# A mixture-of-experts layer on Trainium2: token rows moved by indirect transfers through tables in DRAM, where one-hot products moved them

## The chip, the core and the metric

The kernel runs on one core of one Trainium2 chip. The core has five engines with a queue each: TensorE (PE) for matrix products, VectorE (DVE), ScalarE (ACT), GpSimd (POOL) and SyncE (SP), which only issues transfers. Results of TensorE land in PSUM banks; DVE and ACT read them from there. Transfers are issued from the queue of SP, ACT or POOL and run on 16 shared DMA engines. All data is float32. The metric is the device time of one execution in microseconds (us).

## The reference

Sixteen batches of 64 latent rows (1024 rows of 256 features) go through a two-layer Perceiver: cross-attention, self-attention and a forward layer, then cross-attention over a context of 1024 rows per batch ("L1 xattn"), self-attention ("L1 attn"), and a mixture of experts ("L1 ffn"). The change touches the last:

```python
def _L1_ffn_ref(x, Wr, W1, W2):          # x after _layernorm
    B, S, D, F, E = (8, 512, 256, 1024, 8)
    t = b * s                            # 1024 tokens
    cap = max(math.ceil(t * CAPACITY_FACTOR / E), 1)     # 128
    xf = x.reshape(t, d)
    probs = jax.nn.softmax(xf.astype(jnp.float32) @ Wr, axis=-1)
    eidx = jnp.argmax(probs, axis=-1)
    p_tok = jnp.take_along_axis(probs, eidx[:, None], axis=1)[:, 0]
    onehot = jax.nn.one_hot(eidx, E, dtype=jnp.int32)
    rank_all = jnp.cumsum(onehot, axis=0) - onehot
    rank = jnp.take_along_axis(rank_all, eidx[:, None], axis=1)[:, 0]
    keep = rank < cap
    ...
    xe = xf[dispatch]                    # (8, 128, 256)
    h = jnp.maximum(jnp.einsum('ecd,edf->ecf', xe, W1), 0.0)
    ye = jnp.einsum('ecf,efd->ecd', h, W2)
    ye = ye * (pe * valid.astype(ye.dtype))[:, :, None]
    y = jnp.zeros((t, d), dtype=x.dtype).at[dispatch.reshape(-1)].add(ye.reshape(E * cap, d).astype(x.dtype))
...
x = x + _L1_ffn_ref(_layernorm(x, axis=-1), L1_ffn_Wr, L1_ffn_W1, L1_ffn_W2)
```

Each token goes to the one expert with the highest probability. An expert takes the first 128 tokens that chose it; a token past that keeps its x unchanged.

## The kernel before

The 1024 rows are eight tiles of 128 partitions, held in `xs` for the whole kernel. The stages run one after the other, and each hides work of its neighbours:

- The L0 stage (to about 1160 us) attends over the context and works on the small self-attention of earlier tiles between.
- The L1 loop (`NSTEP` = 64 steps, eight to a token tile, about 12 us a step) attends over the context again. Each step softens the scores of 128 rows (`soften`, `turn_probs`), sends the turned probabilities over SP (`l_pT`), computes keys five steps ahead (`keys`: product, ACT copy, SP transfers `l_ks`, a POOL product at L876, a DVE sum at L877), and sums context rows by the probabilities (`gather`). `weave` lays the gather's products between the other items of the step.
- The L1 self-attention of a finished tile comes as 13 pieces (`make_self_pieces`: 0 norm, 1 turn, 2 to 5 queries and keys, 6 and 7 values, 8 scores and softmax, 9 and 10 turn, 11 attend, 12 output). `SELF_AT` says at which step of the loop each runs: pieces 0 to 7 in the second half of the following tile's steps, 8 to 12 in the first half of the one after. Tiles 6 and 7 finish after the loop, their pieces interleaved by hand with the routing of tiles 0 to 5.

From the L1 loop on every TensorE instruction is pinned (`in_order`, `pin`): TensorE runs them as written, so an instruction whose input is late holds all that follow. On the other engines the framework's scheduler puts the instructions in an order of its own, which then is fixed as well: each engine and each DMA queue works in order.

After the loop, the mixture layer: `route_norm(t)` (L1359) and `route(t)` (L1362) compute the normed rows and eight logits of a tile. When the last tile is done (L1415 to L1446), softmax, choice of expert and slot are computed for all tiles at once: a product with a triangle of ones gives ranks inside a tile, one with ones the counts of the tiles before. Then rows are moved by products with one-hot matrices: `m_send` (L1451, slot equals column) carries the normed rows to their experts (`m_px`, 64 products of 128x512), `m_back` (L1494, made of `m_pb` products) carries results home (`m_pz`, 128 products of 128x256). Per expert there are `m_ph` (hidden layer, ReLU on ACT) and `m_py`. `load_expert` (L1343) issues the two weight matrices of an expert on POOL's queue into the four buffers of `wpool`, two experts ahead.

Helpers named in the profile: `matmul` is L98, `transpose` L102, `copy` L111 (ACT) and L113 (DVE), `load_weight` L118, `inverse_std` L123 and L124, `layer_norm` L132 to L136, `turn_tile`'s copy L148.

Of the kernel before, what the change touches and what calls it, by code (L numbers as in the profile page):

```python
# [41 lines left out]
K6_TRI, K6_IOTA, K6_COL, K6_DESC, K6_SEL = 0, 128, 256, 257, 265  # L42
NK6 = 1289
# [3 lines left out]
def kernel(  # L47
# [9 lines left out]
    k6_in: bass.AP,  # L57
    x_wq: bass.AP,
# [124 lines left out]
    wpool = ctx.enter_context(tc.tile_pool(name="wbig", bufs=4))  # L183
    stc = ExitStack()
# [576 lines left out]
    with ExitStack() as st:  # L761
# [125 lines left out]
        def latents(t):  # L887

            rstd = two.tile([P, 1], F32, tag="ln_rstd", name=f"rstd_l_{t}")
            mv = mv_l.pop(t)
            nc.scalar.activation(rstd, mv[:, 1:2], AF.Sqrt, bias=eps2, scale=1.0 + EPS)
            nc.vector.reciprocal(rstd, rstd)
            xn[t] = one.tile([P, D], F32, tag="xn", name=f"l_xn_{t}")
            nc.vector.tensor_scalar(
                xn[t], xs[:, t, :], mv[:, 0:1], rstd, ALU.subtract, ALU.mult
            )

        def turn_latents(t):
            pt = bank([P, NC, P], f"lnT_l_{t}")
            for c in range(NC):
                transpose(pt[:, c, :], xn[t][:, c * P : (c + 1) * P], ident)
# [184 lines left out]

        SELF_AT = [(8,), (9, 10), (11,), (12,), (0,), (1, 2), (3, 4), (5, 6, 7)]  # L1090
# [4 lines left out]
        def self_pools():  # L1095

            wp = ws.enter_context(tc.tile_pool(name="s_w", bufs=4, side="right"))
            sw["pool"] = ws.enter_context(tc.tile_pool(name="s_one", bufs=1, side="right"))
            sw["ps"] = ps_s
            for name, w in (("q", s_wq), ("k", s_wk), ("v", s_wv), ("o", s_wo)):  # L1100
                sw[name] = load_weight(wp, w, f"w{name}5")

        def self_steps(s):
            t, at = divmod(s, PER_TILE)
            t -= 1 if at >= 4 else 2
            return [self_pieces(t)[n] for n in SELF_AT[at]] if t >= 0 else []
# [6 lines left out]
        def make_self_pieces(t, pool):  # L1113
# [98 lines left out]
            def self_output():  # L1212
# [7 lines left out]
                nc.gpsimd.tensor_tensor(xs[:, t, :], xs[:, t, :], v["xn"][:, 0, :], ALU.add)  # L1220
# [62 lines left out]
        for s in range(NSTEP):  # L1283
# [25 lines left out]
            if t + 1 < NT:  # L1309
# [6 lines left out]
                elif at == 5:  # L1316
                    items.append(lambda: queries(t + 1))
            w = (s - 2) // 2
# [8 lines left out]
        assert not pieces  # L1327
        for c in range(NC):
# [9 lines left out]
    NE, FF = m_w1.shape[0], m_w1.shape[2]  # L1338
# [4 lines left out]
    def load_expert(e):  # L1343
        return load_weight(wpool, m_w1[e], f"w1_{e}"), load_weight(wpool, m_w2[e], f"w2_{e}")

    with ExitStack() as st:
        one = st.enter_context(tc.tile_pool(name="m_one", bufs=1))
        two = st.enter_context(tc.tile_pool(name="m_two", bufs=2))
        k6 = one.tile([P, NK6], F32, tag="k6", name="k6")
        nc.sync.dma_start(out=k6, in_=k6_in)  # L1350
        wr = one.tile([P, NC, NE], F32, tag="wr", name="wr")
        nc.sync.dma_start(out=wr, in_=m_wr.rearrange("(c p) n -> p c n", p=P))
        experts = {e: load_expert(e) for e in range(2)}
        ones = one.tile([P, P], F32, tag="ones", name="ones")
        nc.gpsimd.memset(ones, 1.0)
        xn = one.tile([P, NT, D], F32, tag="xn", name="xn6")
        pl = one.tile([P, NT, NE], F32, tag="logits", name="m_logits")

        def route_norm(t):  # L1359
            layer_norm(two, xs[:, t : t + 1, :], xn[:, t : t + 1, :], f"m_{t}", 1)  # L1360

        def route(t):  # L1362

            hm = turn_tile(two, xn[:, t : t + 1, :], f"m_{t}")
            pr = bank([P, NE], f"m_logits_{t}")
            for c in range(NC):
                matmul(
                    pr, lhsT=hm[:, c, :], rhs=wr[:, c, :], start=(c == 0), stop=(c == NC - 1)
                )
            nc.vector.tensor_copy(pl[:, t, :], pr)  # L1370


        with ExitStack() as tail:
            ps_s = tail.enter_context(tc.tile_pool(name="s_ps", bufs=2, space=bass.MemoryType.PSUM))
            sw["ps"] = ps_s
            sp = tail.enter_context(tc.tile_pool(name="s_last", bufs=1))
            before, last = self_pieces(NT - 2), make_self_pieces(NT - 1, sp)
            last[0]()
            before[8]()
            last[1]()  # L1380
            for n in (2, 3):
                last[n]()
            before[9]()
            for n in (4, 5):
                last[n]()
            before[10]()
            last[6]()
            before[11]()
            last[7]()
            last[8]()  # L1390
            before[12]()
            for t in range(NT - 2):
                route_norm(t)
                route(t)
                if t == 2:
                    last[9]()
                if t == 4:
                    last[10]()
            last[11]()
            route_norm(NT - 2)  # L1400
            route(NT - 2)
            last[12]()
        ws.close()
        route_norm(NT - 1)
        route(NT - 1)
        one = st.enter_context(tc.tile_pool(name="m_big", bufs=1))

        def each(ap):
            return ap.unsqueeze(2).broadcast_to([P, NT, NE])

        red = one.tile([P, NT], F32, tag="red", name="m_red")
        prob = one.tile([P, NT, NE], F32, tag="prob", name="m_prob")
        top = one.tile([P, NT], F32, tag="top", name="m_top")
        hot = one.tile([P, NT, NE], F32, tag="hot", name="m_hot")
        nc.vector.tensor_reduce(red, pl, AX.X, ALU.max)  # L1415
        nc.vector.tensor_tensor(prob, pl, each(red), ALU.subtract)
        nc.scalar.activation(prob, prob, AF.Exp)
        nc.vector.tensor_reduce(red, prob, AX.X, ALU.add)
# [256 lines left out]
```

## Time and profile before

| what | us |
|---|---|
| time, median of 4 runs (lowest, highest) | 2185.66 (2182.41, 2187.97) |
| the profiled execution's own time | 2188.58 |
| its span, first to last instruction | 2186.8 |
| PE, DVE, ACT, POOL busy | 2094.7, 1323.1, 811.4, 311.5 |
| last of the latents' output added to xs | 1989.5 |
| last xs after self-attention | 2040.7 |
| first product of the first expert (m_ph) | 2082.8 |
| last product of m_py ends, about | 2156 |

In the profile a line such as `L98 PE MATMUL m_px<-m_send,xn` names the line of the program, the engine, the operation, and what is written from what. A float32 product is recorded as two matmuls. POOLq, SPq and DVEq are the issuing queues. "Idle before" is the time an engine stood still before the instruction, and `<-` names what ended it. PEclk is the granted clock of TensorE (1.00 is full).

### The profile page before, as it was taken

To read this page: it belongs to the slowest core of one execution; us is meant where nothing else is said; L and a number is where in the kernel's file an instruction comes from. 1 tells how busy PE (TensorE), PEld (TensorE's weight loads), DVE (VectorE), ACT (ScalarE), POOL (GpSimd) and SP (SyncE) were. 2 spreads that over 40 slices of the span, in tenths; PEclk is the share of its full clock that TensorE was granted. 3 is DMA by queue.
4 is the path that set the end of the run, shared out by engine and by line. 5 is a ranking of instruction groups with operands and counts; after the bars stand their busy time and mean duration, and the time that the engine had idled before them with its cause. 6 is when DMAs were issued, how large, how long until landed. Compare 5 with 4: busy or idle time off the path is not lost.

```text
span 2186.8 us, 30787 instructions
## 1 busy us (share of the span) xinstructions
PE 2094.7 (96%) x11016; PEld 1406.9 (64%) x11016; DVE 1323.1 (61%) x2606; ACT 811.4 (37%) x1567; POOL 311.5 (14%) x302
## 2 busy tenths in 40 slices
PE   7899999999999999999998799999999999998799
PEld 4567666667666666666665355666666666676477
DVE  5765656656566575575633768767666767664311
ACT  2222233333342233332434445454545545432110
POOL 2200001001000010010102232222121222211010
PEclk9999999999999999999998999999999999999799
DMA  7343333343333333444322355444444444332052
GB/s 245 87 105 97 84 81 99 85 108 75 83 102 97 74 99 79 109 111 108 79 78 77 80 165 136 106 119 104 103 112 102 116 98 113 95 88 84 0 180 71
DMA packets 150391, 220.48 MB, mean 101 GB/s; under 512 B 34704, under 2 KB 85392, under 8 KB 149984
## 3 DMA queue, kind: packets, MB, share of 16 engines
q1 hardware_dynamic: 142448, 188.00, 34.2%
q0 software_dynamic: 7792, 30.51, 4.1%
q8 instruction: 89, 1.46, 0.3%
q14 instruction: 62, 0.51, 0.1%
HBM read 67.38 MB, written 1.05 MB: 31 GB/s over the span
## 4 chain that ended last, share of the span: by engine, by line
PE 80%; DVE 6%; ACT 5%; issue 3%; SPq 3%; DMA 2%; POOL 1%; DVEq 0%; ACTq 0%; POOLq 0%
PE x_po L98 20%; PE x_s L98 19%; PE l_po L98 8%; PE l_pk L98 7%; PE l_s L98 2%; PE x_pa L98 2%; PE s_pq L98 1%; PE m_py L98 1%; PE m_px L98 1%; PE m_ph L98 1%; PE m_pz L98 1%; PE x_pq L98 1%; SPq L1015 1%; PE x_pv L98 1%; PE s_pk L98 1%
## 5 line engine op out<-in xcount | busy, mean ns | idle before, releaser
L98 PE MATMUL x_s<-ctxT,x_qk 128*128 128x512 f32 x1024 | 472.9, 603 | 10.6 <-ACT pr_x L584 10.6
L98 PE MATMUL x_po<-x_pT,ctx 128*128 128x256 f32 x2048 | 459.3, 382 | 4.2 <-DMA x_pT<-x_pb 4.2
L98 PEld LDWEIGHTS x_po<-x_pT,ctx 128*128 128x128 f32 x2048 | 388.6, 191 | 80.3 <-issue 26.6
L98 PEld LDWEIGHTS x_s<-ctxT,x_qk 128*128 128x128 f32 x1024 | 187.6, 191 | 211.2 <-issue 183.1
L577 DVE TENSOR_REDUCE nmax_x<-x_s 128x1 f32<-128x1024 f32 x128 | 156.0, 1218 | 240.6 <-PE x_s L98 239.6
L98 PE MATMUL l_pk<-l_cnT,wkv 128*128 128x512 f32 x512 | 247.3, 610 | 3.2 <-DVE a_vm L356 1.5
L584 ACT ACTIVATE pr_x<-x_s,shift_x 128x1024 f32<-128x1024 f32 x128 | 142.5, 1114 | 286.9 <-DVE shift_x L581 238.6
L98 PE MATMUL l_po<-l_pT,l_ctx 128*128 128x256 f32 x864 | 232.9, 385 | 7.8 <-DMA l_pT<-l_pb 4.4
L876 POOL TENSOR_TENSOR l_ks<-l_ks,k 128x512 f32<-128x512 f32 x128 | 166.2, 1320 | 424.5 <-DMA l_ks<-l_kr 345.7
L98 PEld LDWEIGHTS l_po<-l_pT,l_ctx 128*128 128x128 f32 x864 | 153.6, 191 | 77.5 <-issue 54.8
L98 PEld LDWEIGHTS l_pk<-l_cnT,wkv 128*128 128x128 f32 x512 | 95.9, 193 | 106.7 <-issue 87.4
L864 ACT ACTIVATE l_kr<-l_pk,l_bkv 128x512 f32<-128x512 f32 x128 | 87.5, 687 | 198.4 <-PE l_pk L98 135.3
L593 DVE STREAM_TRANSPOSE x_pb<-pr_x 128x1024 f32<-128x1024 f32 x128 | 157.3, 1237 | 5.9 <-DMA x_pT<-x_pb 1.9
L618 ACT COPY x_pct<-x_po 128x512 f32<-128x512 f32 x64 | 37.5, 585 | 246.6 <-PE x_po L98 246.6
L865 DVE TENSOR_TENSOR l_kT<-l_kr,k 128x512 f32<-128x512 f32 x128 | 96.2, 754 | 46.8 <-ACT l_kr L864 45.9
L178 DVE TENSOR_SCALAR pr_x<-pr_x,inv_x 128x1024 f32<-128x1024 f32 x128 | 100.2, 782 | 3.2
L983 DVE TENSOR_REDUCE nmax_l<-l_s 128x1 f32<-128x1024 f32 x64 | 75.8, 1219 | 35.6 <-PE l_s L98 35.6
L877 DVE TENSOR_TENSOR l_kT<-l_kT,l_ks 128x512 f32<-128x512 f32 x128 | 92.0, 760 | 4.1 <-POOL l_ks L876 4.1
L584 ACT ACT_TABLE_LOAD x42 | 53.9, 1283 | 105.7 <-DVE shift_x L581 105.6
L1006 DVE STREAM_TRANSPOSE l_pb<-pr_l 128x1024 f32<-128x1024 f32 x64 | 77.7, 1230 | 1.2 <-issue 0.6
L98 PE MATMUL l_s<-l_kT,l_qT 64*64 64x512 f32 x512 | 69.1, 625 | 8.0 <-DVE l_kT L877 8.0
L986 ACT ACTIVATE pr_l<-l_s,nmax_l 128x1024 f32<-128x1024 f32 x64 | 71.5, 1117 | 8.3 <-DVE nmax_l L984 8.0
(302 smaller groups left out, 2657.8 us busy)
## 6 DMA issues: line engine op xcount, KB each, us to landing
x_pT<-x_pb SPq DMA_DIRECT2D x1024, 64.0 KB, 2.0
l_ks<-l_kr SPq DMA_DIRECT2D x256, 128.0 KB, 2.3
l_pT<-l_pb SPq DMA_DIRECT2D x512, 64.0 KB, 2.0
ctx<-in_context_dram SPq DMA_DIRECT2D x32, 512.0 KB, 5.2
w<-in_m_w_dram POOLq DMA_DIRECT2D x16, 1024.0 KB, 5.9
ctxT<-x_cb SPq DMA_DIRECT2D x240, 64.0 KB, 2.0
l_ctx<-in_context_dram SPq DMA_DIRECT2D x27, 512.0 KB, 4.3
l_ctx_spare<-in_context_dram SPq DMA_DIRECT2D x5, 512.0 KB, 4.3
```

The source lines that it names most:

```text
L98: ins = nc.tensor.matmul(*args, **kwargs)
L178: nc.vector.tensor_scalar(pr, pr, inv, None, ALU.mult)
L577: nc.vector.tensor_reduce(nmax, sc, AX.X, ALU.max, negate=True)
L584: nc.scalar.activation(pr, sc, AF.Exp, bias=shift, scale=1.0, accum_out=total)
L593: nc.vector.transpose(blocks[w][:, :, i], pr.rearrange("p (j k s) -> p j k s", j=4, s=32))
L864: nc.scalar.activation(kr[:, i % 2], pk, AF.Identity, bias=bkv[:, i : i + 1])
L865: nc.vector.tensor_tensor(kr2, kr[:, i % 2], k4[:, 0, at], ALU.mult)
L876: nc.gpsimd.tensor_tensor(ks[:, i % 2], ks[:, i % 2], k4[:, 1, at], ALU.mult)
L877: nc.vector.tensor_tensor(kr2, kr2, ks[:, i % 2], ALU.add)
L983: nc.vector.tensor_reduce(nmax, sc[h], AX.X, ALU.max, negate=True)
L986: nc.scalar.activation(pr[h], sc[h], AF.Exp, bias=nmax, scale=1.0, accum_out=total[:, 2 * h : 2 * h + 1])
L1006: nc.vector.transpose(blocks[w][:, :, h].rearrange("p j k s -> p k j s"), pr[h].rearrange("p (k j s) -> p k j s", k=NKT, s=32),)
```

## The change

Routing moves into the L1 loop, tile by tile. `route_norm(t-2)` runs at step 4 of tile t's eight steps, `route(t-2)` at step 5 and a new `place(t-2)` at step 6; tiles 6 and 7 follow after the loop. `place(t)` finds the slot of each token of one tile (t products with ones for the tiles before, one with the triangle) and issues four indirect scatters on POOL's queue, one row per token: the normed row into the table `m_norm`, the probability and the token's number into `m_meta`, the row of `xs` into `m_rest`, all at row 128 x expert + rank; and for a token over capacity the row of `xs` straight to the output. Indices past the end (`NOWHERE`) are dropped. The tables are in DRAM and are filled at `open_routes` from a row of constants.

The experts' phase then reads the tables back with plain transfers (`xr` on ACT's queue, `mm` and `rr` on SP's), turns the rows of an expert on TensorE, computes the two layers one expert ahead, adds the kept rows on DVE and scatters 128 finished rows per expert to the output from POOL's queue. The one-hot matrices and their products are gone. Six experts' weights are loaded ahead, on SP's queue, with a new pool `w_more`; experts 6 and 7 reuse `wpool`. Tile 6's pieces 0 to 3 come two steps later and 4 to 7 after the loop's last step; the order of the last two tiles' pieces is another; the last tile's sum into `xs` runs on DVE.

```diff
+        def open_routes():
+            rt["x"] = one
+            rp = rt["pool"] = routes.enter_context(tc.tile_pool(name="m_route", bufs=1, side="right"))
+            rt["k6"] = rp.tile([P, NK6], F32, tag="k6", name="k6")
+            nc.sync.dma_start(out=rt["k6"], in_=k6_in)
+            rt["wr"] = rp.tile([P, NC, NE], F32, tag="wr", name="wr")
+            nc.sync.dma_start(out=rt["wr"], in_=m_wr.rearrange("(c p) n -> p c n", p=P))
+            rt["hot"] = rp.tile([P, NT, NE], F32, tag="hot", name="m_hot")
+            for name, at, n in (("norm", 0, D), ("rest", 0, D), ("meta", D, 2)):
+                rt[name] = mdram.tile([NTOK, n], F32, tag=name, name=f"m_{name}")
+                nc.gpsimd.dma_start(
+                    out=rt[name], in_=k7_in[:, at : at + n].broadcast_to([NTOK, n])
+                )
+
+        def route_norm(t):
+            rx[t] = rt["x"].tile([P, 1, D], F32, tag="xn", name=f"m_x_{t}")
+            layer_norm(rt["pool"], xs[:, t : t + 1, :], rx[t], f"m_{t}", 1)
+
+        def meta(t):
+            return rt["k6"][:, K6_META + 2 * t : K6_META + 2 * t + 2]
+        def route(t):
+
+            hm = turn_tile(rt["h"], rx[t], f"m_{t}")
+            pr = bank([P, NE], f"m_logits_{t}")
+            for c in range(NC):
+                matmul(
+                    pr, lhsT=hm[:, c, :], rhs=rt["wr"][:, c, :], start=(c == 0), stop=(c == NC - 1)
+                )
+            prob = rt["pool"].tile([P, NE], F32, tag="prob", name=f"m_prob_{t}")
+            nmax = small.tile([P, 1], F32, tag="nmax", name=f"m_nmax_{t}")
+            total = small.tile([P, 1], F32, tag="total", name=f"m_total_{t}")
+            top, hot = meta(t)[:, 0:1], rt["hot"][:, t, :]
+            desc = rt["k6"][:, K6_DESC : K6_DESC + NE]
+            nc.vector.tensor_reduce(nmax, pr, AX.X, ALU.max, negate=True)
+            nc.scalar.activation(prob, pr, AF.Exp, bias=nmax, scale=1.0, accum_out=total)
+            soft_norm(prob, total, f"m_{t}")
+            nc.vector.tensor_reduce(top, prob, AX.X, ALU.max)
+            nc.vector.scalar_tensor_tensor(hot, prob, top, desc, ALU.is_equal, ALU.mult)
+            nc.vector.tensor_reduce(total, hot, AX.X, ALU.max)
+            nc.vector.tensor_scalar(hot, desc, total, None, ALU.is_equal)
+
+        def place(t):
+
+            pool, hot = rt["pool"], rt["hot"]
+            pr = bank([P, NE], f"m_rank_{t}")
+            for k in range(t):
+                matmul(
+                    pr, lhsT=rt["k6"][:, K6_ONES : K6_ONES + P], rhs=hot[:, k, :],
+                    start=(k == 0), stop=False,
+                )
+            matmul(
+                pr, lhsT=rt["k6"][:, K6_TRI : K6_TRI + P], rhs=hot[:, t, :],
+                start=(t == 0), stop=True,
+            )
+            keep = pool.tile([P, NE], F32, tag="keep", name=f"m_keep_{t}")
+            at = pool.tile([P, NE], F32, tag="at", name=f"m_at_{t}")
+            one = small.tile([P, 2], F32, tag="one", name=f"m_one_{t}")
+            idx, idx2 = (
+                pool.tile([P, 1], mybir.dt.int32, tag=f"idx{k}", name=f"m_idx{k}_{t}")
+                for k in range(2)
+            )
+            nc.vector.scalar_tensor_tensor(
+                keep, pr, float(P), hot[:, t, :], ALU.is_lt, ALU.mult
+            )
+            nc.vector.tensor_tensor(at, pr, rt["k6"][:, K6_PLACE : K6_PLACE + NE], ALU.add)
+            nc.vector.tensor_tensor(at, at, keep, ALU.mult)
+            nc.vector.tensor_reduce(one[:, 0:1], at, AX.X, ALU.add)
+            nc.vector.tensor_scalar(idx, one[:, 0:1], NOWHERE, None, ALU.add)
+            nc.vector.tensor_reduce(one[:, 1:2], keep, AX.X, ALU.add)
+            nc.vector.tensor_scalar(
+                idx2, one[:, 1:2], NOWHERE, meta(t)[:, 1:2], ALU.mult, ALU.add
+            )
+            for k, dst, src in (
+                (idx, rt["norm"], rx.pop(t)[:, 0, :]), (idx, rt["meta"], meta(t)),
+                (idx, rt["rest"], xs[:, t, :]), (idx2, out, xs[:, t, :]),
+            ):
+                pin(nc.gpsimd.indirect_dma_start(
+                    out=dst, out_offset=bass.IndirectOffsetOnAxis(ap=k, axis=0),
+                    in_=src, in_offset=None, bounds_check=NTOK - 1, oob_is_err=False,
+                ))
...
         def self_steps(s):
             t, at = divmod(s, PER_TILE)
-            t -= 1 if at >= 4 else 2
-            return [self_pieces(t)[n] for n in SELF_AT[at]] if t >= 0 else []
+            items = []
+            if t >= 2 and at in (5, 6):
+                items.append(lambda: (route if at == 5 else place)(t - 2))
+            n = SELF_AT[at]
+            t1 = t - (1 if at >= 4 else 2)
+            if t1 == NT - 2:
+
+                n = {6: (0,), 7: (1, 2, 3)}.get(at, ())
+            return items + ([self_pieces(t1)[k] for k in n] if t1 >= 0 else [])
 
...
                 nc.vector.tensor_tensor(v["xn"][:, 0, :], po, v["xn"][:, 0, :], ALU.add)
-                nc.gpsimd.tensor_tensor(xs[:, t, :], xs[:, t, :], v["xn"][:, 0, :], ALU.add)
+
+                eng = nc.vector if t == NT - 1 else nc.gpsimd
+                eng.tensor_tensor(xs[:, t, :], xs[:, t, :], v["xn"][:, 0, :], ALU.add)
...
+            if t >= 2 and at == 4:
+                items.append(lambda: route_norm(t - 2))
...
+        for n in (4, 5, 6, 7):
+            self_pieces(NT - 2)[n]()
...
+    def load_expert(e, pool):
+        ws = []
+        for k, w in enumerate((m_w1[e], m_w2[e])):
+            ws.append(pool.tile([P, w.shape[0] // P, w.shape[1]], F32, tag="w", name=f"w{k + 1}_{e}"))
+            nc.sync.dma_start(out=ws[k], in_=w.rearrange("(c p) n -> p c n", p=P))
+        return ws
...
+        more = st.enter_context(tc.tile_pool(name="w_more", bufs=8))
+        experts = {e: load_expert(e, wpool if e < 2 else more) for e in range(6)}
...
+            rt["x"] = rt["h"] = two
             before, last = self_pieces(NT - 2), make_self_pieces(NT - 1, sp)
             last[0]()
             before[8]()
-            last[1]()
-            for n in (2, 3):
+            for n in range(1, 9):
                 last[n]()
-            before[9]()
-            for n in (4, 5):
+            for n in (9, 10, 11, 12):
+                before[n]()
+            route_norm(NT - 2)
+            for n in (9, 10):
                 last[n]()
-            before[10]()
-            last[6]()
-            before[11]()
-            last[7]()
-            last[8]()
-            before[12]()
-            for t in range(NT - 2):
-                route_norm(t)
-                route(t)
-                if t == 2:
-                    last[9]()
-                if t == 4:
-                    last[10]()
+            route(NT - 2)
             last[11]()
-            route_norm(NT - 2)
-            route(NT - 2)
+            place(NT - 2)
             last[12]()
+            route_norm(NT - 1)
+            route(NT - 1)
+            place(NT - 1)
...
+        xr = one.tile([P, NE, D], F32, tag="xr", name="m_xr")
+        rr = one.tile([P, NE, D], F32, tag="rr", name="m_rr")
+        mm = one.tile([P, NE, 2], F32, tag="mm", name="m_mm")
+        to = one.tile([P, NE], mybir.dt.int32, tag="to", name="m_to")
+        rows3 = rt["norm"].rearrange("(e p) d -> p e d", p=P)
+        for e0, e1 in ((0, 1), (1, 3), (3, NE)):
+            nc.scalar.dma_start(out=xr[:, e0:e1, :], in_=rows3[:, e0:e1, :])
+        nc.sync.dma_start(out=mm, in_=rt["meta"].rearrange("(e p) k -> p e k", p=P))
+        nc.sync.dma_start(out=rr, in_=rt["rest"].rearrange("(e p) d -> p e d", p=P))
+        nc.vector.tensor_copy(to, mm[:, :, 1])
+
...
+        turn_rows(0)
+        turn_rows(1)
+        hidden(0)
+        for e in range(NE):
+            hidden(e + 1)
+            turn_rows(e + 2)
+            w2 = experts.pop(e)[1]
...
+            res = two.tile([P, D], F32, tag="res", name=f"m_res_{e}")
             nc.vector.scalar_tensor_tensor(
+                res, py, mm[:, e, 0:1], rr[:, e, :], ALU.mult, ALU.add
+            )
+            nc.gpsimd.indirect_dma_start(
+                out=out, out_offset=bass.IndirectOffsetOnAxis(ap=to[:, e : e + 1], axis=0),
+                in_=res, in_offset=None, bounds_check=NTOK - 1, oob_is_err=False,
+            )
+            if e < 2:
+                experts[e + 6] = load_expert(e + 6, wpool)
```

## The prediction

> **What bounds the kernel now.** I read the page from the top, then the chain in order of time from 1975 us on, then a table by stretch, then the groups and waits of POOL and SP, which the change loads. The page gives one full engine:
>
> ```profile
> span 2186.8 us, 30787 instructions
> ...
> PE 2094.7 (96%) x11016; PEld 1406.9 (64%) x11016; DVE 1323.1 (61%) x2606; ACT 811.4 (37%) x1567; POOL 311.5 (14%) x302
> ...
> PEclk9999999999999999999998999999999999999799
> ```
>
> TensorE is busy 96% of the span; its clock drops only in the last slices. The table by stretch splits the L1 loop (1284 to 1984), the last two token tiles (to 2041), and the mixture layer after:
>
> ```profile
> 1284.00:1984.00 700.00, 681.25 (x4252) 455.24 (x4253) 470.98 (x847) 334.08 (x694) 160.84 (x133) 1.00 0.45 112
> 1984.00:2041.00 57.00, 45.01 (x476) 36.80 (x474) 26.64 (x75) 19.86 (x30) 8.10 (x9) 0.79 0.19 66
> ```
>
> Columns are length, then busy us of PE, PEld, DVE, ACT, POOL, then clock. In the loop PE idles 18.75 us of 700, so any product added there shows; DVE is at 67%. In the second stretch PE idles 12 us and its clock is 0.79: it waits on the last tiles' softmax. From there everything lies on one chain:
>
> ```profile
> 2043.42 0.63 PE m_logits L98 x4
> 2044.07 0.18 DVE m_logits L1370
> ...
> 2051.99 1.87 PE m_st L102 x8
> 2053.85 5.06 PE m_px L98 x10
> ...
> 2061.19 21.73 PE m_px L98 x50
> 2082.92 3.57 PE m_ph L98 x32
> 2086.49 1.91 PE m_pb L98 x4
> 2088.40 3.65 PE m_py L98 x16
> ...
> 2155.97 27.64 PE m_pz L98 x128
> 2183.63 0.48 DVE m_res L1515
> ```
>
> The experts' own products (m_ph, m_py) take 7.2 us each; m_px, m_pb and m_pz are the one-hot moving. POOL's rows and SP's waits, for the new transfers:
>
> ```profile
> L118 POOL DMA_DIRECT2D wk<-in_s_wk_dram x1 | 0.7, 721 | 0.0
> L118 POOL DMA_DIRECT2D wo<-in_s_wo_dram x1 | 0.9, 922 | 0.0
> L245 POOL DMA_DIRECT2D aw<-in_a_w_dram x1 | 0.5, 534 | 1.0 <-DMA wkT<-in_x_wk_dram 1.0
> L210 POOL MEMSET eps<- 128x1 f32 x1 | 0.1, 98 | 0.0
> ...
> POOL l_ks L876 <- DMA l_ks<-l_kr: 345.7, 45, 12.3
> ...
> SPq L873 <- DVE l_kT L877: 18.9, 11, 2.6
> ...
> out_dram<-m_res SPq DMA_DIRECT2D x8, 128.0 KB, 1.7
> ```
>
> POOL waits 345.7/45 = 7.7 us a step for l_ks: that is the room for its new work. SP already waits at times for the buffer that POOL's l_ks product helps to free.
>
> **What leaves the path.** After the last xs (2040.7): m_px, 2053.85 to 2082.92, 29.1; m_st 1.9; m_pb 8 x 1.91 = 15.3; m_pz 27.7; the batch routing from logits to slots, 2044.07 to 2051.99, 7.9. Sum 81.9 us. The DVE work that went with them (m_send 9.2, m_back 12.0) was hidden under PE and is worth nothing more.
>
> **What comes onto the path there.** Routing of the last tile, from logits to row index: maximum 0.25, table load 1.28 and exponential with its sum 0.5, some twelve small DVE steps at 0.23 (the m_hot, m_red rows), the rank product 0.5: 5.3. The first scatter's issue X, and its landing 2.0 (between 1.7, the out rows, and the 2.0 of the 64 KB moves). Reload of the first expert's rows from the table: 2.0. Two transposes and the copy, as lnT_m and hT_m ran: 1.2. Transposes of the rows for the six experts whose turn lies between products, 6 x 0.43: 2.6. PE starts the experts after an idle stretch: s_pq there took 3.78 and s_pk 2.72 instead of 1.95 at 1995 us: 2.6. The result leaves by a POOL scatter, X + 2.0, where SP took 2.7: X - 0.7. Sum 15.0 + 2X.
>
> X is one indirect scatter of 128 rows on POOL, and no row shows one. Lower end 0.53, the smallest plain transfer on POOL. Upper end: every row handled like an instruction of its own, 128 x 0.098 (the MEMSET of 128x1) = 12.5. I take 1.5: the row nearest in kind is the plain POOL transfer with 1 KB runs, 0.92, and reading the list of indices is added as one more such fixed start, 0.53. Stage net: 15.0 + 3.0 - 81.9 = -63.9.
>
> **The last two tiles (1984 to 2041).** Routing of tiles 0 to 5 leaves, but it filled the wait on tile 7's softmax; in its place come tile 6's turn, attention and output. Tile 7 still waits: tile 6's output, its norm, its route (transposes, copy, logits, 1.6) and its place sit ahead of tile 7's attention and output in PE's written order, and each needs DVE and ACT first, with Sqrt, Exp and Gelu tables (1.28 each) taking turns. Walking the order with these durations, tile 7's xs comes 3 us sooner. Bounds: 0 if each of these waits ends as late as now, 12 if PE's idle here goes. The last addition on DVE (0.42) rather than POOL (0.72) is in the 3. Pieces 4 to 7 of tile 6 now come after the loop, in front of the last gather: the same products, and the 1.3 us wait for l_pT at 1975 is filled.
>
> **The loop gains work.** For tiles 0 to 5: transposes 0.41 and logits 0.61, 6 x 1.02 = 6.1. `place(t)` has t+1 products of 128x8; two such take 0.61, so 21 x 0.305 = 6.4. In `route` the logits follow the transposes with only a DVE copy between: 0.52 where DVE was free (the m_logits rows), and about 0.7 more behind a busy DVE: 6 x 1.2 = 7.3. Sum 20 on PE, at worst all on the path; at best its 18.75 us of idle takes half: +10. DVE gets per tile norm 1.2, copy 0.42, seven steps of route and seven of place at 0.23, 4.8 in all, ACT two table loads, Sqrt and Exp, 3.4: I take nothing for them, since DVE (67%) and ACT (48%) have room under PE; without that cover they would cost up to 6 x 8.2 = 49.
>
> POOL gets four scatters per tile, pinned, and stands still until the indices come. Behind them on its queue are the next step's l_ks product and tile t+1's s_pr scaling; for l_ks wait DVE's key sum, then SP's next l_ks transfers and, in SP's order, l_pT, which PE's gather needs. 4X fits into 7.7 while X is under 1.9, so at 1.5 nothing is late. Above, 4 x 6 = 24 us per further us of X if all of it passes through.
>
> **At nothing.** The table fills (three POOL transfers, 0.9 each, once, in a 7.7 us gap). Constants and m_wr earlier on SP, 2 x 0.6, beside a wait of SP. Expert loads moved from POOL to SP: 16 issues of 0.6 with SP idle. Six experts' 12.6 MB start when the last latent products free the buffers, about 1990; at four loads in 18.0 us (the s_w loads) that is 54 us, 2044, while expert 0's are first and the others follow at 7.6 us each. At 5.9 us a load (the m_w rows) the last lands at 2061, when expert 5 starts past 2090. The reload on ACT's queue (three issues) waits behind nothing.
>
> **Sum.** 2186.8 - 63.9 - 3 + 20 = 2139.9. The profiled execution took 2188.58, 1.8 around its span, and stands 2.9 above the median 2185.66: forecast 2139.9 + 1.8 - 2.9 = 2139, 2.1% faster.
>
> **A rule against it.** POOL's rows show transfers beside DVE work at their normal 0.72 to 0.92, at 1284.8 to 1287.9, though the only DVE work beside them read PSUM. The Trainium skill, page SBUF — State Buffer, section "SBUF: two separate sides", says that a transfer issued from POOL can't write its descriptors while DVE runs an operation that takes both shared ports, and gives some 620 ns alone against some 3100 beside a DVE copy. By that, an estimate of X = 4.0 in the loop, the sum would be 2139 + 24 x 2.1 = 2189: no gain. I keep the row's view, since DVE's queue holds such operations only part of the time.
>
> **Rivals.**
> *Scatters dear on POOL (slower).* Place: POOL between two l_ks products. Each us of X above 1.9 costs 24 in the loop and 2 at the end. The gain of 46.7 is used up at X = 1.9 + 45.9/26 = 3.7. At 12.5: 254 in the loop, 22 at the end, and the experts run at POOL's 12.5 instead of PE's 7.6 (+39): 2139 + 315 = 2454. For it: no row shows X, POOL is in order, SP's waits show that l_ks is close. Against: 7.7 us of room, plain transfers under 1 us with eight times the runs.
> *Middle price.* X of 2 to 3.7, or copies and routing waiting on DVE and ACT: 2142 to 2186. For it: s_xn on DVE varied from 0.37 to 1.34 us, so DVE's queue is not free.
> *Loop covers more.* Half the 20 hidden and the 12 us of PE's idle before 2041 gone: 2139 - 10 - 9 = 2120. For it: 18.75 us of idle; against: PE's order is written by hand, and route stalls it.
> *No change.* The reload chain and the late routing eat all 82: it would take 47 us more than counted, 12 at the end and 35 in the loop; only the first rival offers that.
>
> **How the numbers follow.** A measurement of this kernel tells about 0.2% (4 us) from no change. Chances: main case, 2122 to 2155, 0.42; loop covers more, 2105 to 2122, 0.14; middle price, to 2181, 0.21; dear scatters, above 2190, 0.20; within 0.2%, 0.03. Faster 0.77, same 0.03, slower 0.20. For 8 in 10 the range takes the first three and the beginning of dear scatters (X to about 4.7): 2105 to 2212; the likeliest alone has 2122 to 2155.
>
> **What would show it.** Right: m_px, m_pb, m_pz gone, experts' products 7.6 us apart; first m_ph some 14 us after the last xs; L1 loop about 20 us longer with POOL's scatter rows near 1.5; l_ks products no later than now. Wrong: scatter rows above 2 us; PE waiting for l_pT or l_kT after each `place`; waits of PE on hT_m in the loop above 2 us; POOL, not PE, setting the distance between experts.

## The result and the profile after

The changed kernel takes 2190.84 us (median; 2185.9 to 2195.72) where the kernel before, measured beside it, takes 2187.78 (2181.54 to 2195.03). The ratio is 1.0015 with a 95% interval of 1.001 to 1.002: no gain, where 2.1% was forecast and 2139.0 us. The profiled execution took 2189.98 us, with a span of 2188.2.

The page of the kernel after, the lines that answer to those of before:

```profile
span 2188.2 us, 30690 instructions
...
PE 2039.0 (93%) x10868; PEld 1378.1 (63%) x10868; DVE 1317.0 (60%) x2666; ACT 817.5 (37%) x1582; POOL 337.5 (15%) x327
...
PE   5599999999999999999998888999999999999868
...
PEclk8799999999999999999998999999999999999879
DMA  9533334334333343344433246544444443433621
```

and the same two rows of the kernel before:

```profile
PE   7899999999999999999998799999999999998799
DMA  7343333343333333444322355444444444332052
```

TensorE does 56 us less, as meant, and the span is 1.4 us longer. So some 57 us of new idle time must be found. The first row shows most of it without any further view: PE has 5, 5 in its first two slices (0 to 109 us), where before it had 7, 8. Nothing of the mixture layer was meant to run there.

The table by stretch of the kernel after (length, busy us of PE, PEld, DVE, ACT, POOL, then clock, share of the DMA engines' time, GB/s); the last two rows are the L1 loop and the last two tiles, cut at the same work as in the forecast's table:

```profile
0.00:30.00 30.00, 19.63 (x102) 15.74 (x103) 9.39 (x35) 6.28 (x20) 13.07 (x22) 0.89 0.95 338
30.00:60.00 30.00, 12.34 (x61) 6.28 (x59) 4.58 (x11) 3.63 (x12) 0.00 (x0) 0.77 1.12 88
60.00:100.00 40.00, 22.25 (x62) 12.42 (x63) 28.34 (x54) 5.21 (x9) 8.88 (x7) 0.75 0.38 100
1317.00:2044.30 727.30, 698.72 (x4322) 465.67 (x4322) 493.36 (x960) 341.93 (x715) 181.06 (x154) 0.99 0.44 109
2044.30:2100.70 56.40, 41.12 (x454) 34.02 (x451) 20.27 (x53) 20.50 (x27) 8.77 (x9) 0.79 0.59 208
```

and the same first stretches of the kernel before:

```profile
30.00:60.00 30.00, 28.13 (x118) 16.37 (x118) 28.14 (x62) 7.65 (x17) 5.38 (x3) 1.00 0.46 128
60.00:100.00 40.00, 34.12 (x129) 21.88 (x128) 31.05 (x68) 10.74 (x17) 10.91 (x13) 0.96 0.37 91
```

Between 30 and 60 us the DMA engines are busy all the time (1.12; before 0.46) and move less (88 GB/s; before 128). What is on them, the groups and POOL's timeline say: the three fills of the tables are not issued at 1284 us, where `open_routes` stands in the program, but at 17 to 24 us. They depend on nothing, so the scheduler put them into the first free place on POOL's queue.

```profile
L1109 POOL DMA_DIRECT2D m_norm<-in_k_dram x1 | 0.8, 832 | 0.1
L1109 POOL DMA_DIRECT2D m_rest<-in_k_dram x1 | 0.8, 765 | 2.5 <-DMA wv<-in_x_wv_dram 2.5
L1109 POOL DMA_DIRECT2D m_meta<-in_k_dram x1 | 0.8, 755 | 3.0 <-DMA wo<-in_x_wo_dram 3.0
...
L1176 POOL DMA_INDIRECT out_dram<-xs,m_idx x8 | 8.2, 1019 | 97.8 <-DVE m_idx L1167 70.1 <-DVE m_one L1166 20.9 <-DVE m_idx L1169 6.8
L1176 POOL DMA_INDIRECT m_norm<-m_x,m_idx x8 | 7.8, 976 | 2.4 <-issue 2.4
...
L1540 POOL DMA_INDIRECT out_dram<-m_res,m_to x8 | 7.7, 967 | 61.9 <-DVE m_res L1537 39.4 <-issue 22.5
```

Issuing a fill costs POOL 0.8 us, where 0.9 was forecast. An indirect scatter costs 0.97 to 1.02 (busy us, mean ns); no row has one over 1.11. What a fill does after its issue is in the waits of TensorE:

```profile
PE x_s L100 <- ACT pr_x L587: 43.0, 11, 33.1
PE lnT_e L104 <- DMA m_xr<-m_norm: 10.1, 1, 10.1
...
PE m_logits L100 <- DVE hT_m L150: 7.6, 8, 1.2
...
PE s_pk L100 <- ACT l_kr L867: 4.1, 5, 1.6
PE lnT_m L104 <- ACT l_kr L867: 3.8, 5, 0.8
```

One wait of 33.1 us in x_s, at the start. Placing the same instructions of both profiles side by side gives the whole account (us, rounded from hundredths; x_out, a_out and l_out are the outputs of L0's cross-attention, L0's self-attention and L1's cross-attention, each taken at the start of its addition to xs on DVE, the last xs at its end):

| from, to | before | after | difference | forecast |
|---|---|---|---|---|
| start to first xs<-x_out | 197.8 | 229.7 | +31.9 | 0 |
| to first xs<-l_out | 1153.7 | 1154.8 | +1.1 | 0 |
| first to last xs<-l_out (L1 loop) | 638.0 | 665.2 | +27.3 | +20 |
| to the last xs | 51.2 | 50.6 | -0.6 | -3 |
| last xs to the end | 146.1 | 87.8 | -58.3 | -63.9 |
| sum | 2186.8 | 2188.2 | +1.4 | -46.9 |

The end of the kernel, in the timeline of the kernel after:

```profile
2099.97 0.42 DVE L1324 TENSOR_TENSOR xs<-xs,s_xn 128x256 f32<-128x256 f32 x1
...
2107.46 0.97 POOL L1176 DMA_INDIRECT out_dram<-xs,m_idx  x1 [6.78 <-DVE m_idx L1169]
...
2108.74 0.97 POOL L1176 DMA_INDIRECT m_norm<-m_x,m_idx  x1 [0.30 <-issue]
...
2111.20 1.35 ACTq L1497 DMA_DIRECT2D m_xr<-m_norm  x3
...
2116.62 1.39 PE L104 MATMUL lnT_e<-ident,m_xr 128*128 128x128 f32 x4 [10.08 <-DMA m_xr<-m_norm]
...
2119.72 0.17 DVE L1500 CAST m_to<-m_mm 128x8 int32<-128x8 f32 x1 [12.05 <-DMA m_mm<-m_meta]
2119.80 0.75 DVE L150 COPY hT_e<-lnT_e 128x256 f32<-128x256 f32 x2
...
2120.28 9.47 PE L100 MATMUL m_ph<-hT_e,w 128*128 128x128 f32 x64 [2.27 <-DVE hT_e L150]
```

m_px, m_st, m_pb and m_pz are gone and the experts follow each other at 7.2 us, so this part of the change does what it should. The first m_ph comes 19.9 us after the last xs is written, where 14 were forecast.

### The profile page after: what moved, and what is told of

It is laid out like the page before. It is cut to its first block, busy times and chain, and to the rows that moved or that the text cites. A ratio compares the mean times of both kernels' runs of the same rounds, so it can differ in the third digit from the quotient of the medians.

```text
span 2188.2 us, 30690 instructions
## 1 busy us (share of the span) xinstructions
PE 2039.0 (93%) x10868; PEld 1378.1 (63%) x10868; DVE 1317.0 (60%) x2666; ACT 817.5 (37%) x1582; POOL 337.5 (15%) x327
## 5 line engine op out<-in xcount | busy, mean ns | idle before, releaser
L100 PEld LDWEIGHTS x_po<-x_pT,ctx 128*128 128x128 f32 x2048 | 388.5, 191 | 80.3 <-issue 27.3
```

Source lines behind the costliest of these rows:

```text
L100: ins = nc.tensor.matmul(*args, **kwargs)
```

## The experiments

Theory at this point: the fills stop the start, because each reads one row of 1 KB (or 8 bytes) 1024 times and the 16 DMA engines are held by it. Rivals: the fills would cost the same wherever they stand; or the start is late for another reason.

**f1: the fills at their written place.**

```diff
-                nc.gpsimd.dma_start(
+                pin(nc.gpsimd.dma_start(
                     out=rt[name], in_=k7_in[:, at : at + n].broadcast_to([NTOK, n])
-                )
+                ))
```

> The three table fills are pinned behind the GpSimd work that is written ahead of them, so they run at about 1284 us, in front of the s_w loads, and no longer at 17 us. Theory (the fills stop the start): norm_x of tile 0 waits for the context loads, which wait behind the fills; the 31.9 us that the changed kernel loses before its first l_out come back, the first xs<-x_out lies at about 198 us again, and the time is 2190.8 - 31.9 = 2159 us (2154 to 2165), ratio 0.987 to the kernel before. Rival 1 (the fills cost their 30 us of transfer wherever they run): the start is as before, but l_ks and l_pT transfers stand behind the fills at 1284 and the loss comes back there: 2180 to 2191. Rival 2 (the start is late for another reason than the fills, such as another order of GpSimd's or SyncE's work): first xs<-x_out stays at about 230, 2191.

Measured: 2190.03 us, ratio 1.0007 (0.9995 to 1.002). The start is back (first xs<-x_out at 199.6), and the loss has moved: from the last xs<-a_out to the first xs<-l_out it takes 129.4 us where before took 93.2. Rival 1 holds. The stretches of f1 from 1290 us on:

```profile
1290.00:1310.00 20.00, 2.37 (x17) 0.93 (x15) 1.20 (x2) 0.00 (x0) 0.00 (x0) 0.64 0.88 93
1310.00:1330.00 20.00, 9.75 (x26) 4.47 (x26) 4.77 (x5) 0.00 (x0) 2.48 (x2) 0.67 0.94 198
1330.00:1350.00 20.00, 11.33 (x35) 7.49 (x36) 7.85 (x17) 10.61 (x22) 2.52 (x3) 0.66 0.60 166
```

and the first of them in the kernel before:

```profile
1290.00:1310.00 20.00, 15.99 (x67) 9.38 (x66) 11.05 (x12) 7.05 (x15) 5.40 (x4) 0.83 0.88 264
```

TensorE works 2.4 us of the first 20, where the kernel before worked 16.0. In f1's waits between 1285 and 1350 us it is POOL's l_ks that stands still for its transfers, three times, 58.0 us in all:

```profile
POOL l_ks L879 <- DMA l_ks<-l_kr: 58.0, 3, 28.2
```

Before, such a wait was 7.7 us on the average. So the scheduler's move is not the fault: the fills cost 32 to 36 us at either place, since both have transfers behind them that TensorE needs. What the same fills would cost at a place with less behind them was not tried.

**f2: the fills alone, in the kernel before.**

```diff
...
         def self_pools():
...
+            for name, at, n in (("norm", 0, D), ("rest", 0, D), ("meta", D, 2)):
+                table = mdram.tile([NTOK, n], F32, tag=name, name=f"m_{name}")
+                nc.gpsimd.dma_start(
+                    out=table, in_=k7_in[:, at : at + n].broadcast_to([NTOK, n])
+                )
...
```

> The kernel before with the three fills alone added, into tables that nothing reads; they stand on GpSimd's queue where the changed kernel has them, behind the first x_prod at 17 us. Theory (the fills stop the start): the whole loss without any of the routing: 2187.8 + 31.9 = 2220 us (2214 to 2225), ratio 1.0146. Rival 2 (another cause): 2188, ratio 1.000.

Measured: 2220.69 us (2213.86 to 2221.44), ratio 1.0153 (1.0131 to 1.0176), 32.1 us over the kernel before. The fills alone make the loss, with nothing of the routing there.

**f3: only the fill of m_meta left at the start, the two of 1 MB at 1284 us.**

```diff
+                fill = nc.gpsimd.dma_start(
                     out=rt[name], in_=k7_in[:, at : at + n].broadcast_to([NTOK, n])
                 )
+                if name != "meta":
+                    pin(fill)
```

> The changed kernel with the two fills of 1 MB (m_norm, m_rest) at 1284 us and only m_meta's 1024 pieces of 8 bytes left at the start. If the loss goes by the number of pieces (1024 of 3072), a third is left: first xs<-x_out at about 208, 2159 + 11 = 2170 us. If the 8-byte pieces are what holds the queues: 2186 to 2191. If it goes by bytes or by the 1 KB pieces: 2159 us, as with all three late.

Measured: 2191.15 us. As a total this looks like the second case, and the landmarks say that it is not: the first xs<-x_out is at 202.5 (4.7 us late), and 28.0 us are lost at 1290 us, where the two large fills now stand. The expectation was written as if 1284 us were free of charge, which f1 refutes. What the run tells is the split: the 8 KB table takes 3 to 9 us at the start (a start without fills lies between 193.2 and 199.6 in these runs), the two of 1 MB about 28.

**f4: the same place and the same pieces of 1 KB, from 1024 different rows.**

```diff
+                rows8 = "(t p) d -> p t d"
+                if n == D:
+                    nc.gpsimd.dma_start(
+                        out=rt[name].rearrange(rows8, p=P), in_=x.rearrange(rows8, p=P)
+                    )
...
```

> The changed kernel with all three fills at the start, but m_norm and m_rest filled from the 1024 different rows of x in DRAM, in pieces of 1 KB as before; the filling's values are never used. If reading one row of DRAM 2048 times is what makes the fills slow (a packet of about 4 KB took 0.84 us between 30 and 45 us, 0.17 between 15 and 30), the two pass at the loads' rate, 2 MB at about 360 GB/s or 6 us: first xs<-x_out at about 204, 2165 us (2159 to 2172). If it is the writing to DRAM or the piece of 1 KB, nothing changes: about 230, 2191 us.

Measured: 2168.19 us (2167.48 to 2168.66), ratio 0.9912 (0.989 to 0.9934); first xs<-x_out at 208.0. So 22 of the 32 us go with the source being one row. (The edit also writes the rows in another order, by partition; that was not tried by itself.) The queues of the DMA engines between 30 and 45 us (packets, MB, share of 16 engines; q0 is POOL's, q1 SP's), first the kernel after:

```profile
q0 software_dynamic: 260, 1.00, 91.2%
q1 hardware_dynamic: 261, 0.26, 7.1%
```

then f4:

```profile
q0 software_dynamic: 491, 1.77, 87.0%
q1 hardware_dynamic: 765, 0.76, 14.9%
```

A packet of q0, about 3.8 KB, holds an engine for 15 x 16 x 0.912 / 260 = 0.84 us when it repeats one row, 0.43 from different rows. The weights loaded into SBUF by the same queue between 15 and 30 us in the kernel before take 0.17 (1017 packets, 73.8%). SP's context loads get what is left: 0.26 MB in these 15 us, 2.38 in the kernel before.

**f5: whole copies, in the L0 stage.** m_norm and m_rest are copied from x in 16 pieces of 64 KB, m_meta from a table of 1024x2 constants, one each in the steps of tiles 2, 3 and 4.

```diff
+    def fill_table(name):
+        src = k7_in if name == "meta" else x
+        tables[name] = mdram.tile([NTOK, src.shape[1]], F32, tag=name, name=f"m_{name}")
+        pin(nc.gpsimd.dma_start(out=tables[name], in_=src))
...
+        if at == 12 and 2 <= t < 5:
+            fill_table(("norm", "rest", "meta")[t - 2])
...
```

> The changed kernel with other fills: m_norm and m_rest are copied whole from x (1 MB each in 16 pieces of 64 KB), m_meta from a table of 1024x2 numbers (8 KB, 16 pieces), one each in the L0 stage of tiles 2, 3 and 4, where the 16 DMA engines are 30% busy. Theory (it is the one row read 2048 times that costs, not the tables): the start is as before (first xs<-x_out at 198), the first xs<-l_out lies at 1352 to 1356, and 2190.8 - 32.5 = 2158 us (2154 to 2164). Rival (some 6 us are lost at the place of each large copy, since x_pT's transfers wait behind 64 KB pieces): 2165 to 2172.

Measured: 2157.78 us (2154.31 to 2165.44), ratio 0.9869 (0.9843 to 0.9895): the theory's 2158. The fills in f5's list of transfers, with the time from issue to landing at the end:

```profile
m_norm<-in_x_dram POOLq DMA_DIRECT2D x1, 5.9
...
m_meta<-in_k_dram POOLq DMA_DIRECT2D x1, 8.0 KB, 2.0
```

A table of 1 MB lands 5.9 us after its issue here, 17 in f4, 33 to 39 from one row (m_rest, in f1, f2, f3 and the kernel after; m_norm, issued ahead of it, 27 in f2). The slower ones had other transfers beside them, and f5 changes the place together with the size of the pieces, so these runs do not say which of the two took the last 10 us. The Trainium skill, page DMA: Bandwidth & Descriptors, section "Anatomy of one DMA — SWDGE (gpsimd) path", fits 2.0 us plus the bytes at 436 GB/s, an estimate of 4.4 us for 1 MB; the whole copy comes near it. For the other two forms it would be an error of 13 and of 23 to 34 us, and the measured times decide.

The loss at the start is settled with that. What is open is the loop, 7 us over the forecast. Theory P: work and stalls on TensorE. Rival: the scatters on POOL's queue.

**f6: f5 without the scatters of tiles 0 to 5. f7: f5 with two items in place of `route`. f8: f5 without any routing of tiles 0 to 5.** In f6 and f8, and in f10 below, the rows of these tiles reach no table: the three leave out a part of the layer and serve for the time alone.

```diff
 # f6, in place(t)
+                if t < NT - 2:
+                    continue
                 pin(nc.gpsimd.indirect_dma_start(
 # f7, in self_steps(s)
+                if at == 5:
+                    items.append(lambda: route_turn(t - 2))
                 items.append(lambda: (route if at == 5 else place)(t - 2))
 # f8, in self_steps(s); route_norm likewise
-            if t >= 2 and at in (5, 6):
+            if t >= NT and at in (5, 6):
```

> f5 without the four indirect scatters of tiles 0 to 5 (their rows reach no table, and the text says so); norm, route and place of these tiles stay. Of the loop's growth of 27 us (first to last xs<-l_out, 638 to 665), theory P (work and stalls on TensorE) gives GpSimd's scatters nothing: 664 us in the loop, total as f5. Rival (the scatters, 4 x 1.3 us per tile on GpSimd's queue, hold back l_ks, l_pT or the buffer of l_xn): the loop is 10 to 20 us shorter, 645 to 655.

> f5 with the routing's transposes and its logits as two items of the woven list, so that four products l_po stand between them. Theory P: the wait of the logits on hT_m (5 x 1.2 us in the trace) goes, and with it part of the slower products behind it (s_pq 303 ns each against 277, l_po 387 against 384): the loop is 7 to 11 us shorter than f5's, 654 to 658. Rival (DVE, GpSimd or SyncE is what the loop waits for): the wait moves to another row and the loop stays at 664.

> f5 without norm, route, place and scatter of tiles 0 to 5 (their rows reach no table, m_hot is zero for them). If the routing is the whole of the loop's growth: first to last xs<-l_out 638 to 640 us as before, total 26 us under f5. If something else of the change lengthens the loop (pieces 4 to 7 of tile 6 moved, the layout of SBUF, the tables' pool): it stays above 645.

| run | median us | first to last xs<-l_out |
|---|---|---|
| f5 | 2157.78 | 666.0 |
| f6, no scatters | 2147.32 | 664.2 |
| f7, split | 2149.47 | 659.9 |
| f8, no routing | 2125.34 | 637.8 |
| before | 2188.11 | 638.0 |

f8: the routing is the whole growth of the loop; moved pieces and the layout cost nothing. f7 takes 6.0 us out of the loop, a little less than expected, since four l_po are still too short a cover: m_logits waits 3.8 us for hT_m where f5's waited 6.0. Its products behind the wait are faster, s_pq 283 ns against 298: the granted clock stands at 0.5 for 3.4 us once in f7's loop and three times in f5's. f6 is not clear by itself: 1.8 us in the profiled loop, 10.5 by the medians, and f5's own runs spread over 11. (f6's profiled execution is its slowest, with five such stretches of 3.4 us.) That led to f9 to f11.

**f9: everything mended; f10: f9 without the scatters of tiles 0 to 5; f11: f9 with them twice.** Beside f5's fills, f9 puts the transposes of the routing two items ahead of the logits, keeps a running sum of `m_hot`, so that `place` has two products and not t+1, and issues m_norm's scatter first.

```diff
+            if t >= 2 and at == 5:
+                items.insert(1, lambda: route_turn(t - 2))
...
-            for k in range(t):
+            if t:
                 matmul(
-                    pr, lhsT=rt["k6"][:, K6_ONES : K6_ONES + P], rhs=hot[:, k, :],
+                    pr, lhsT=rt["k6"][:, K6_ONES : K6_ONES + P], rhs=rt["sum"][:, t - 1, :],
...
+            first = scatter(idx, rt["norm"], rx.pop(t)[:, 0, :])
+            with tc.issue_after(first.ins):
+                scatter(idx, rt["meta"], meta(t))
...
 # f10
+            if t < NT - 2:
+                return
 # f11, behind the four
+                if t < NT - 2:
+                    scatter(idx, rt["norm"], xn_t)
...
```

> f5's fills, and in the loop: the routing's transposes two items ahead of the logits (l_pk, l_pt and four l_po between them), the rank from a running sum of m_hot (two products of 128x8 per tile in place of t+1: 9 fewer over tiles 2 to 5, and 5 and 6 fewer at the end), and m_norm's scatter ahead of out's, rest's and meta's. From f7's 2149.5: the rest of the wait on hT_m (3.8 us in its trace), 9 x 0.25 = 2.3 us of rank products, and at the end one scatter (1.27 us) less ahead of the reload: 2149.5 - 3.8 - 2.3 - 1.3 = 2142 us (2136 to 2148), ratio 0.979. Rival: the waits move to s_pk and lnT_m, which wait for a bank that ACT's l_kr frees: 2148 to 2151.

> f9 without the four scatters of tiles 0 to 5 (their rows reach no table). In f6 the profiled loop was 1.8 us shorter without them, the median of the runs 10 us. If the scatters cost the loop nothing (GpSimd stands idle for 10 us ahead of them): as f9, within 3 us. If they hold back l_ks, l_pT or l_xn: 6 to 12 us under f9, with shorter waits of TensorE on l_kr and DVE on l_xn.

> f9 with the four scatters of tiles 0 to 5 issued twice each (the same rows to the same places), eight in a row, some 10.3 us on GpSimd's queue per tile. By the forecast's rule (room of 7.7 us a step, 4 us of queue per us of X beyond it): 10.3 - 7.7 = 2.6 us late per tile, 6 x 2.6 = 16 us over f9 if all of it passes through to TensorE. If the room in front of l_ks is larger than 7.7: as f9, within 3 us. If already the first four pass through in part: 8 to 31 us.

Measured: f9 2134.36 us (2133.11 to 2135.55), ratio 0.9754 (0.9741 to 0.9767); f10 2128.1; f11 2178.07 (2172.21 to 2181.12). In the loop 647.5, 642.8 and 692.4 us. f9 is 7.6 us better than expected: its waits on hT_m are gone and those of lnT_m (4.0 us in f7) too, which the rival had counted as staying; s_pq is at 278 ns, as before the change, and the granted clock reads 1.00 through the whole loop. It is 2.5% under the kernel before; of the kernels that compute the whole layer only f12, below, is as fast. Its three edits were not tried one by one.

The first four scatters per tile cost 6.3 us by the medians (4.7 in the loop), f10's second case; the second four cost 43.7 (44.9), more than any case of f11's expectation. TensorE's waits in the loop, f9:

```profile
PE s_pk L100 <- ACT l_kr L876: 4.0, 5, 0.9
PE l_po L100 <- DVE l_pct L1065: 3.9, 5, 1.6
```

and f11:

```profile
PE s_pk L100 <- ACT l_kr L876: 16.3, 5, 4.3
PE l_pt L104 <- ACT l_kr L876: 12.3, 5, 3.1
```

In f10 the wait of s_pk is 0.7 in all. So the forecast's room of 7.7 us on POOL's queue was not there: four scatters (5.1 us) already reach TensorE a little, and of the further 5.1 us per tile nearly all arrives (24.6 us more waiting in five tiles, 4.9 each). POOL's timeline shows why, here in the kernel after:

```profile
1520.94 1.11 POOL L1176 DMA_INDIRECT out_dram<-xs,m_idx  x1 [10.62 <-DVE m_idx L1167]
...
1524.94 0.97 POOL L1176 DMA_INDIRECT m_rest<-xs,m_idx  x1 [0.30 <-issue]
1525.93 2.50 POOL L879 TENSOR_TENSOR l_ks<-l_ks,k 128x512 f32<-128x512 f32 x2
```

POOL stands 10.62 us waiting for the indices, and when the four scatters end at 1525.9 the next l_ks product starts in the same moment, without a wait for its transfers. It is so behind the scatters of all five tiles in the loop, and behind the eight of f11. Only the time between the indices and the next l_ks is room, and the wait before the indices is none. The rest of the 7.5 us per tile in f11 is slower products (s_pk 339 ns against 277), and nearly all of it lies where the granted clock is at 0.5: in each of the five tiles that happens at these waits, for 6.8 us in the first and 10.2 in each of the others, such as here:

```profile
1606.60:1616.80 10.20, 7.13 (x26) 6.14 (x27) 6.69 (x14) 6.09 (x13) 0.00 (x0) 0.50 0.26 56
```

The SBUF rule that the prediction weighed, some 3100 ns for a POOL transfer beside a DVE operation that takes both shared ports, is not seen in the kernel after: its 40 scatters took 967 to 1108 ns. The test is a weak one, since only 13 of the 40 had a DVE instruction beside them.

**f12: f9 with one DVE instruction moved,** the cast of the result's row numbers behind the copies of the first experts' rows.

```diff
-        nc.vector.tensor_copy(to, mm[:, :, 1])
...
         turn_rows(1)
+        pin(nc.vector.tensor_copy(to, mm[:, :, 1]))
         hidden(0)
```

> f9 with one DVE instruction moved: the cast of the result's row numbers (m_to from m_mm) stands behind the two copies hT_e of the first experts. In f9's trace lnT_e of expert 0 ends at 2060.7 and its copy starts only at 2063.66, behind the cast, which waits for m_mm to land. Theory (DVE's order holds the first expert back): first m_ph 16.5 to 17 us after the last xs in place of 19.4, total 2134.4 - 2.7 = 2131.7 us (2129 to 2134). Rival (the copy waits for something else, such as the second expert's rows): still 19.4, 2134.

Measured: 2134.18 us (2132.14 to 2135.43), ratio 0.9745 (0.9732 to 0.9758). In the trace the theory holds: from the start of the last xs to that of the first m_ph 17.1 us, in f9 19.4; from the last xs to the end 84.5, in f9 86.4. The total is where the rival had it, and doesn't resolve 2 us: f12's profiled execution had reached its first xs<-l_out 3.5 us later than f9's, in code that is the same in both.

f12's timeline there:

```profile
2064.72 0.42 DVE L150 COPY hT_e<-lnT_e 128x256 f32<-128x256 f32 x1 [8.83 <-PE lnT_e L104]
...
2067.42 0.17 DVE L1549 CAST m_to<-m_mm 128x8 int32<-128x8 f32 x1 [1.26 <-DMA m_mm<-m_meta]
```

## Why the prediction was wrong

The forecast was 47 us of gain in the span and the result 1.4 us of loss: 48.3 us to explain. Four steps hold them.

- **"At nothing. The table fills (three POOL transfers, 0.9 each, once, in a 7.7 us gap)": the step that failed, 31.9 us of the 48 at the start, 33.0 with the 1.1 up to the loop.** It priced the issue (0.8 measured) and not the transfer. The issue's duration says nothing of a transfer in 3072 pieces whose source is one row. The fills were also taken at their written place, while the scheduler could move them; f1 shows that this second error alone would have changed nothing. f2 gives the cost by itself, 32.1 us. f4 gives 22 of it to the repeated row. The rest goes in f5, with larger pieces at another place, and 3 to 9 of it belong to m_meta's pieces of 8 bytes (f3).
- **The loop, +27.3 for +20.** Three of its terms were about right. Transposes and logits took 2.2 + 2.9 us in five tiles (6.1 for six; forecast 6.1), the rank 3.7 us for 15 products (5.2 for 21; forecast 6.4), the wait on hT_m 6.0 in five tiles (7.2; forecast 7.3). Missing were slower products: over the loop l_po took 4.6 us, s_pq 3.5 and s_pk 0.5 more than before, at the same counts. For s_pq it is the clock. Behind the two waits on lnT_m and hT_m (0.8 and 1.2 us) the granted clock falls to 0.5 for 3.4 us in three of the five tiles, and s_pq's first 16 records there take 328, 405 and 410 ns each on the average, 280 in the two tiles without the fall. Of l_po's share some 0.8 us lies in these stretches, and the runs do not settle the rest. Also missing were 7.9 us of waits on l_kr, in s_pk and lnT_m, against which some 5 us of waits of s_pq on hT_s and lnT_s on l_kr went. f9 takes the waits on hT_m and lnT_m away, its clock stays at 1.00 and s_pq is back at its old duration; s_pk still waits 4.0 us on l_kr.
- **The end, -58.3 for -63.9.** The rows behind the 81.9 us removed are gone, and the account of the end closes at that price. Of the 18.0 added, three were too small or missing: the reload from issue to landing took 5.4 us and not 2.0; out's scatter stood ahead of m_norm's (1.3); the copy of the first expert's rows stood behind the cast on DVE's queue (2.3, f12). Two X at 0.97 and not 1.5 give 1.1 back. That makes 5.9 us, where 5.6 were measured.
- **The last two tiles, -0.6 for -3.** The result lies by the bound of 0 named there, that tile 7's waits end as late as before; no run tries this stretch by itself.

The granted clock in the kernel after, first in a tile without the fall, then in two with it (the third number from the end of a line):

```profile
1505.00:1509.00 4.00, 3.73 (x27) 3.29 (x28) 3.00 (x11) 0.89 (x6) 1.18 (x1) 1.00 0.68 170
1609.20:1612.60 3.40, 3.40 (x14) 2.67 (x14) 2.19 (x8) 0.36 (x2) 1.25 (x2) 0.50 0.62 118
1817.40:1820.80 3.40, 3.33 (x16) 2.99 (x15) 3.40 (x5) 0.00 (x0) 2.28 (x2) 0.51 0.65 186
```

X was taken at 1.5 us and is 0.97 to 1.02, so the scatters were not dear, and the rival that the prediction gave most weight on the slower side did not occur. The measured time still lies inside the range given for 8 in 10, in the part that was put there for dear scatters: that is luck. The room of 7.7 us that the break-even of X = 1.9 stood on was wrong as well, and only the small X hid it: f11 loses 44 us to f9 where that rule gave 16. "No change" stood in the prediction as a rival needing "12 at the end and 35 in the loop"; the amount was right and the place was not, because the whole account looked only at stages that the edit names.

## What to carry to other kernels

A transfer has two prices: the issue on its queue, and the time its packets hold the DMA engines that all other transfers need; ask both of every transfer, a one-off fill included, and ask who waits behind it. Fill a table from as many different rows as it has, in large pieces, at a time when the DMA engines are idle, and state that time in the program: an instruction that depends on nothing is put where the scheduler likes. On a queue that works in order, the room for new work is the time between the arrival of its input and the next instruction's, not the mean idle time of the engine. Where products are slow, ask the granted clock in stretches as short as they are: a mean over a tile hides a fall of 3.4 us.

## What was not expected of the hardware

- Copying one DRAM row of 1 KB 1024 times into DRAM took 27 to 39 us from issue to landing, 1024 different rows in pieces of 1 KB 17, the same 1 MB in 16 pieces, at another place, 5.9. Why one row is slower than many was not tried further; the per-packet times (0.84 and 0.43 us) are all that the runs show.
- An indirect scatter of 128 rows holds POOL for 0.97 us whether the row has 8 bytes (m_meta, 969 ns) or 1 KB (m_norm, 976 ns), 1.27 us from start to start in a row of four.
- The granted clock falls for a few us behind waits that are short, and a mean hides it: it reads 0.98 to 1.00 over the tiles of the loop in the kernel after, and 0.5 in three stretches of 3.4 us inside. All of these stand behind a wait of 0.8 us and one of 1.2 us shortly after it. Two further tiles with the same two waits have no fall, and the loops of f9 and of the kernel before, with single waits of 0.8 to 1.6 us, have none. Why it comes in some tiles and not in others the runs do not show.
